# Reading skewed score rows back in two half-height transfers of 128 columns, in a four-layer graph network kernel

## The chip, the cores and the metric

The kernel runs on one core of a Trainium2 chip, as one launch. The metric is device time in microseconds (us) from the first to the last instruction. Before the change three runs gave 2887.09, 2887.32 and 2894.89 us, median 2887.32 us. The profiled execution of the same kernel spans 2889.8 us.

The engines are named as in the profile: PE multiplies matrices (PEld is its weight load), DVE and ACT do elementwise work on vectors, POOL is a slower general engine, and SP only issues transfers. Transfers are carried out by 16 DMA engines, which take a queue's packets in order.

## The reference: what is computed

The input is 128 graphs of 128 nodes with 128 features, and a 0/1 adjacency matrix for each. Four graph layers follow one another, each added to its input after a layer norm and a relu. The change lies in the second layer, which builds attention from pairs of nodes:

```python
D = jnp.abs(x[:, :, None, :] - x[:, None, :, :])
h = jnp.einsum('bijc,oc->bijo', D, W1) + b1
# batch norm of h over all b, i, j, then leaky relu with slope 0.01
s = jnp.einsum('bijo,uo->biju', h, W2)[..., 0] + b2[0]
s = jnp.where(A_init > 0, s, NEG)
A = jax.nn.softmax(s, axis=-1)
y = jnp.einsum('bij,bjc->bic', A, x)
```

For every pair of nodes (i, j) of a graph there is one score, s. It is symmetric in i and j, because D is an absolute difference. So half of the pairs are enough, if the other half is put in place afterwards.

## The kernel before, in words

**Stages.** The first stage (to about 1620 us) computes the first layer, and for the second layer the hidden values h of all pairs, which it stores to DRAM as tensors named hp. Since the batch norm needs statistics over everything, the scores can only be finished in a second pass. That pass is the middle stage (about 1620 to 2400 us): it loads hp back as tiles named z, finishes the scores, and computes attention and the layer's output. The last stage does layers three and four.

**Half of the pairs, by distance.** For node i the kernel keeps only the pairs with the nodes i + 1 to i + 64, counted cyclically (`KH` is 32, so 2 * KH is 64). With the diagonal, a row has 1 + 64 scores. They lie in the tile sk (128 nodes x 4 batches x 65), by distance and not by column.

**Rows of scores.** To turn distance into column, the row of node i is written to DRAM starting at column i. The DRAM buffer rows has 128 rows of `ROW` = 192 columns per batch; the step from row to row in the write is `ROW + 1`, which shifts each row by one. This is `to_rows`, L994. Row i then covers the columns i to i + 64. Those from 128 on stand for columns 0 to 63, since the distance is cyclic. The buffers are set to zero once at the start, and what no row covers stays zero. Two buffers serve the groups by turns (`slots`).

`from_rows`, L1001, reads all 192 columns of all 128 rows back as the tile u. `folded`, L1012, adds the columns 128 to 191 onto the columns 0 to 63. u then holds one half of the score matrix; PE transposes it (`turned("put", t["u"])`, L986), and `scores` adds u and its transpose, L1016, and masks it, L1017. After that come the softmax, the products and the stores of `stored`, L1048 and L1050.

**The order of work.** In the middle stage it is written out by hand. One slot handles one batch (`slot(b)`); four batches are a group, whose chain of steps is spread over twelve slots by `at(slot, place, work)`. In its slot a batch's z tiles get a scale, bias and leaky relu on ACT and DVE (L944, L948, L962), PE multiplies them by the score weights (L919), and two z tiles for later are fetched (`fetch`, L911). Ten z tiles of 1 MB are in the ring (`FETCHED`). For group g, with s0 = 4g + 9, the write to rows is issued in slot s0 - 4, the read in slot s0 - 2, the fold is in slot s0, and the scores are in slot s0 + 1.

**Queues.** All these transfers are issued by SP, in program order: in a group 8 z, one sk, one x load, one u, one x store and (for 24 of 32 groups) one store of y. The read of u waits for the write of sk to land, because it reads what that wrote. What stands behind the read in the program is not issued before it. The issues also take eight completion semaphores by turns, so that each waits for the transfer eight places ahead of it to have landed.

Of the kernel before, what the change touches and what calls it, by code (L numbers as in the profile page):

```python
# [14 lines left out]
OP = mybir.AluOpType  # L15
AX = mybir.AxisListType

P = 128
# [9 lines left out]
KH = 32  # L28
# [138 lines left out]
def tile_gnn_stack(ctx: ExitStack, tc: tile.TileContext, a: dict, out: bass.AP):  # L167
    nc = tc.nc
# [681 lines left out]
    with tc.tile_pool(name="c1", bufs=1) as c1, tc.tile_pool(name="p1", bufs=2) as p1:  # L850
# [22 lines left out]
                                       add_k[:, :, 4:8], op0=OP.mult, op1=OP.add)  # L873


        slots = []
        zero = c1.tile([P, G, ROW], F32, name="zero")
        nc.vector.memset(zero, 0.0)
        for n in range(2):
            rows = dr.tile([G, P, ROW], F32, tag=f"rows{n}", name=f"rows{n}")  # L880
# [4 lines left out]
        for n in range(2):  # L885
            t = c1.tile([P, G, 1 + 2 * KH], F32, name=f"sk{n}")
# [86 lines left out]
        def chain(g):  # L973

            rows = slots[g % 2]
            t = {}
# [21 lines left out]

            def from_rows():
                t["u"] = p1.tile([P, G, ROW], F32, name="u")  # L1000
                nc.sync.dma_start(t["u"], rows.rearrange("g i r -> i g r"))  # L1001

            def normed():
                t["h"] = pre_norm(p1, t["x"], MV1[:, g], RS1[:, g])
# [3 lines left out]
                nc.gpsimd.tensor_tensor(t["x1"], t["x"], over_group(bt), OP.add)  # L1008

            def folded():  # L1010
                u = t["u"]
                nc.vector.tensor_tensor(u[:, :, 0:2 * KH], u[:, :, 0:2 * KH], u[:, :, P:], OP.add)  # L1012

            def scores():
                t["e"] = p1.tile([P, G, P], F32, name="e1")
# [35 lines left out]

            at(s0 - 4, "s", to_rows)
            at(s0 - 2, "s", from_rows)
            at(s0, "e", normed)
            at(s0, "p", lambda: turned("pt", t["h"]))
            at(s0, "l", folded)
            at(s0 + 1, "am", lambda: copied("hT", "pt"))
            at(s0 + 1, "p", lambda: turned("put", t["u"]))
# [511 lines left out]
```

## Time and profile before

| stage, us from the start | DMA, GB/s | PE busy | DVE busy | ACT busy |
|---|---|---|---|---|
| 0 to 1630 | 202 | 1397.8 of 1630 | 1491.1 | 1415.4 |
| 1700 to 2330 | 409 | 546.3 of 630 | 539.5 | 501.9 |
| 2400 to 2890 | 49 | 416.3 of 490 | 387.1 | 386.3 |

The table is from the busy times by stretches. A busy engine is one that executes; waiting is not counted. Matmuls are pipelined and the ends of their records are modelled, so PE's share is a rough one. The DMA share is the mean busy share of the 16 DMA engines.

Over the whole span PE is busy for 85%, DVE for 87% and ACT for 83%, but these are means over stages that differ: only the middle stage loads the DMA engines fully. The chain of work that ended last passes through the transfers z<-hp (7%), rows<-sk (7%) and u<-rows (5% of the span).

### The profile page before, as it was taken

The numbers are of one execution on the slowest core, as the hardware profiler recorded it, in microseconds if no ns is written. First come the engines' busy times: TensorE is split into PE (matmuls) and PEld (weight loads), VectorE is DVE, ScalarE is ACT, GpSimd is POOL, SyncE is SP. The second block draws the span as 40 slices with busy tenths as digits, with TensorE's granted clock in tenths as the row PEclk, the third lists the DMA queues.
The fourth block names the chain that finished last, engine by engine and source line by source line (L and its number), as shares of the span: only waits on it lengthen the run. The fifth ranks groups of instructions, "written<-read, shape, count | busy, mean of one in ns | idle before, by whom it ended". The sixth has DMA issues, their size and how long they took to land.

```text
span 2889.8 us, 41921 instructions
## 1 busy us (share of the span) xinstructions
PE 2469.7 (85%) x14517; PEld 1185.7 (41%) x14517; DVE 2520.0 (87%) x4949; ACT 2392.2 (83%) x2811; POOL 1729.1 (60%) x1613
## 2 busy tenths in 40 slices
PE   1899899999898989898989688888888886998897
PEld 1333333333333333333333234444444444777675
DVE  5799999999999999999999578888888885987886
ACT  1799998989899999999999678777877774988886
POOL 2899989898989899898988001101111104665552
PEclk8899999999999999999999899999999997999998
DMA  5555545454544444454544999999999971111210
GB/s 200 201 202 221 204 190 204 190 204 190 204 193 200 195 199 200 193 207 186 215 171 204 368 408 408 410 409 409 410 410 410 408 283 54 45 59 63 63 34 27
DMA packets 180083, 653.83 MB, mean 226 GB/s; under 512 B 30992, under 2 KB 99472, under 8 KB 129680
## 3 DMA queue, kind: packets, MB, share of 16 engines
q1 hardware_dynamic: 179280, 646.80, 56.3%
q10 hardware_dynamic: 576, 4.19, 0.4%
q8 instruction: 119, 1.95, 0.3%
q14 instruction: 108, 0.88, 0.1%
HBM read 338.14 MB, written 312.80 MB: 225 GB/s over the span
## 4 chain that ended last, share of the span: by engine, by line
PE 36%; ACT 23%; DMA 20%; DVE 12%; issue 5%; POOL 3%; SPq 0%; DVEq 0%; ACTq 0%; POOLq 0%
PE hp L595 17%; ACT d L624 11%; DMA z<-hp 7%; DMA rows<-sk 7%; PE hp L598 5%; ACT hs L608 5%; DMA u<-rows 5%; DVE d L585 3%; PE pv L1292 2%; ACT o L717 2%; PE ps L919 1%; ACT h L1176 1%; DVE z L962 1%; PE po L741 1%; POOL rs L221 1%
## 5 line engine op out<-in xcount | busy, mean ns | idle before, releaser
L585 POOL TENSOR_TENSOR d<-xe 128x2048 f32<-128x2048 f32 x256 | 1074.0, 4201 | 86.2 <-PE hp L595 65.7
L595 PE MATMUL hp<-d,w1T 128*64 128x512 f32 x4096 | 1019.2, 621 | 123.1 <-ACT d L624 65.4
L624 ACT ACTIVATE d<-d 128x2048 f32<-128x2048 f32 x384 | 730.9, 1922 | 9.2 <-POOL d L585 5.0
L585 DVE TENSOR_TENSOR d<-xe,xp 128x2048 f32<-128x2048 f32 x256 | 579.9, 2265 | 28.6 <-PE xp L660 21.2
L608 ACT COPY hs<-hp 128x1024 f32<-128x1024 f32 x512 | 512.1, 1017 | 80.2 <-PE hp L598 43.3
L595 PEld LDWEIGHTS hp<-d,w1T 128*64 128x64 f32 x4096 | 290.9, 142 | 691.7 <-issue 465.3
L1008 POOL TENSOR_TENSOR x<-x,bt 128x512 f32<-128x512 f32 x32 | 43.7, 1366 | 684.7 <-DMA x<-x 684.7
L615 DVE BATCH_NORM_STATS2 st<-hs 128x6 f32<-128x512 f32 x512 | 348.8, 681 | 51.6 <-ACT hs L608 51.6
L616 DVE BATCH_NORM_STATS2 st<-hs 128x6 f32<-128x512 f32 (+1 forms) x512 | 328.7, 642 | 0.0
L962 DVE SCALAR_TENSOR_TENSOR z<-z 128x2048 f32<-128x2048 f32 x128 | 297.0, 2320 | 22.8 <-ACT z L944 22.8
L944 ACT ACTIVATE z<-z,bias,scale 128x2048 f32<-128x2048 f32 x128 | 267.3, 2088 | 18.8 <-DMA z<-hp 18.8
L948 ACT ACTIVATE zr<-z,bias,scale 128x2048 f32<-128x2048 f32 x128 | 267.4, 2089 | 9.7 <-DMA z<-hp 7.5
L598 PE MATMUL hp<-both_t,xw 128*64 128x512 f32 x1024 | 266.2, 594 | 0.0
L919 PE MATMUL ps<-z,w2z 128*32 128x512 f32 x1024 | 141.7, 626 | 83.2 <-DVE z L962 83.2
L926 PEld LDWEIGHTS pk<-pick,su 128*128 128x128 f32 x1024 | 125.7, 193 | 139.9 <-DVE su L940 103.0
L926 PE MATMUL pk<-pick,su 128*128 128x16 f32 x1024 | 138.2, 267 | 25.8 <-DVE su L940 24.7
L1292 PE MATMUL pv<-wr,e 128*128 128x128 f32 x1024 | 148.4, 293 | 10.7 <-DVE e L1269 6.1
L1292 PEld LDWEIGHTS pv<-wr,e 128*128 128x128 f32 x1024 | 133.8, 204 | 19.7 <-issue 3.8
L919 PE MATMUL ps<-z,w2l 128*32 128x512 f32 x1024 | 139.1, 612 | 0.6 <-DMA z<-hp 0.6
L919 PE MATMUL ps<-zr,w2r 128*32 128x512 f32 x1024 | 139.0, 615 | 0.4 <-ACT zr L948 0.4
L598 PEld LDWEIGHTS hp<-both_t,xw 128*64 128x64 f32 x1024 | 78.1, 138 | 143.1 <-issue 142.5
L1269 DVE SCALAR_TENSOR_TENSOR e<-e,ps 128x512 f32<-128x512 f32 x160 | 106.8, 678 | 28.7 <-ACT ps L1266 27.9
(266 smaller groups left out, 3855.5 us busy)
## 6 DMA issues: line engine op xcount, KB each, us to landing
hp<-hs SPq DMA_DIRECT2D x128, 2048.0 KB, 6.3
z<-hp SPq DMA_DIRECT2D x256, 1024.0 KB, 14.8
x<-x SPq DMA_DIRECT2D x128, 256.0 KB, 4.8
u<-rows SPq DMA_DIRECT2D x32, 384.0 KB, 11.6
x<-in_x_dram SPq DMA_DIRECT2D x32, 256.0 KB, 3.0
adj<-in_adj_dram SPq DMA_DIRECT2D x32, 256.0 KB, 3.4
out_dram<-x SPq DMA_DIRECT2D x32, 256.0 KB, 2.5
agg<-a SPq DMA_DIRECT2D x30, 256.0 KB, 3.8
```

Source lines behind the costliest of these rows:

```text
L585: eng.tensor_tensor(d, ahead, x[:, None, None, :].to_broadcast([P, 2, KC, P]), OP.max if t == BY_MAX else OP.subtract)
L595: nc.tensor.matmul(hp[64 * hh:64 * hh + 64, c:c + 512], w1T2 if by_max else w1T, d[:, hh, c:c + 512], start=True, stop=not by_max, skip_gr ...
L598: nc.tensor.matmul(hp[64 * hh:64 * hh + 64, c:c + 512], XW[i // NT // 2][:, i // NT % 2, :], both_t.rearrange("p h k i -> p h (k i)")[:, h ...
L608: nc.scalar.copy(halves[b][:, t, :], linear.pop(i))
L615: nc.vector.bn_stats(st[:, 2 * t, :], hs[:, 0:512])
L616: nc.vector.bn_stats(st[:, 2 * t + 1, :], hs[:, 512:1024 - P * last])
L624: nc.scalar.activation(diffs[i], diffs[i], AF.Abs)
L919: nc.tensor.matmul(ps[32 * c:32 * c + 32, :], w[:, w0:w0 + 32], v[:, 512 * c:512 * c + 512], start=j0 == 0, stop=w is w2r, skip_group_chec ...
L944: nc.scalar.activation(z0, z0, AF.Identity, bias=bias1, scale=scale1[:, 0:1])
L948: nc.scalar.activation(zr, z1, AF.Relu, bias=bias1, scale=scale1[:, 0:1])
L962: nc.vector.scalar_tensor_tensor(z0, z0, 0.01, z0, op0=OP.mult, op1=OP.max)
L1292: nc.tensor.matmul(t[pv][:, k % 2, hd, :], t[e][:, hd, :], flat[:, at:at + P], start=True, stop=True)
```

## The change

Row i covers columns i to i + 64. Rows 0 to 63 therefore never reach beyond column 127, and rows 64 to 127 never use a column below 64. So each half of the rows needs only 128 of the 192 columns. The change reads them as two transfers: rows 0 to 63 with columns 0 to 127, and rows 64 to 127 with columns 64 to 191. It is there to move 256 KB per group in place of 384 KB.

The fold changes with it. For the lower half of the rows there is nothing to fold. For rows 64 to 127 the columns 0 to 63 of u are no longer read from DRAM, so the columns 128 to 191 are copied there in place of being added to zeros; the copy runs on 64 partitions. The tile u, the DRAM buffers and the write of the rows stay as they are.

```diff
             def from_rows():
                 t["u"] = p1.tile([P, G, ROW], F32, name="u")
-                nc.sync.dma_start(t["u"], rows.rearrange("g i r -> i g r"))
+                for i in (0, 64):
+                    nc.sync.dma_start(t["u"][i:i + 64, :, i:i + P],
+                                      rows[:, i:i + 64, i:i + P].rearrange("g i r -> i g r"))
...
             def folded():
-                u = t["u"]
-                nc.vector.tensor_tensor(u[:, :, 0:2 * KH], u[:, :, 0:2 * KH], u[:, :, P:], OP.add)
+                u = t["u"][64:]
+                nc.vector.tensor_copy(u[:, :, 0:2 * KH], u[:, :, P:])
```

## The prediction

> **What bounds the kernel now.** I read the page's slices first, to find which stage holds the change. The edited lines run only in the middle stage, where scores become attention weights; it is the block of nines in the DMA row, slices 22 to 31.
>
> ```profile
> DMA  5555545454544444454544999999999971111210
> GB/s 200 201 202 221 204 190 204 190 204 190 204 193 200 195 199 200 193 207 186 215 171 204 368 408 408 410 409 409 410 410 410 408 283 54 45 59 63 63 34 27
> ```
>
> In that stage the 16 DMA engines move 408 to 410 GB/s; before it half that, after it a seventh. A table by stretches of 160 us inside it (columns: time, busy PE, PEld, DVE, ACT, POOL, PE clock, DMA share, GB/s):
>
> ```profile
> 1860.00:2020.00 160.00, 136.84 (x1062) 65.61 (x1062) 137.72 (x209) 127.50 (x89) 15.35 (x12) 1.00 1.03 409
> ```
>
> PE and DVE are busy for 86%, ACT for 80%, the DMA engines for all of it. (The share passes 1 because packets overlap a little.) In a table by single microseconds, from 1937 to 1986 us, the DMA share never falls below 0.94, so the queue does not run dry between bursts. Next the waits, of the engines and of the DMA-issuing queue SP, over 1700 to 2300 us (total, times, longest):
>
> ```profile
> DVE u L1012 <- DMA u<-rows: 46.5, 26, 3.3
> SPq L1001 <- DMA rows<-sk: 100.8, 25, 5.4
> SPq L994 <- DMA z<-hp: 48.6, 24, 2.4
> ```
>
> No engine waits for the large z transfers themselves; they are fetched ten ahead. What compute waits for is u, which stands behind those z transfers in the one queue: 1.9 us a group. The same window's transfers (KB each, us to landing), and the fold beside a one-source DVE operation of known size:
>
> ```profile
> z<-hp SPq DMA_DIRECT2D x202, 1024.0 KB, 14.7
> u<-rows SPq DMA_DIRECT2D x25, 384.0 KB, 11.6
> rows<-sk SPq DMA_DIRECT2D x25, 130.0 KB, 13.3
> L1012 DVE TENSOR_TENSOR u<-u 128x256 f32<-128x256 f32 x26 | 11.1, 426 | 46.5 <-DMA u<-rows 46.5
> L244 DVE TENSOR_SCALAR hn<-hn 128x512 f32<-128x512 f32 x25 | 10.7, 427 | 0.9
> ```
>
> Landing times of 11 to 15 us for transfers of 0.3 to 2.5 us at 409 GB/s mean some 10 us of work already queued. A group of four batches takes 23.76 us (the issues at L994 go from 1723.9 to 2294.2 in 24 steps). So this stage lasts as long as its DMA work does; taking DMA time out shortens it, taking engine time out does not.
>
> [...] The new rows are exactly 512 B, the old ones 768 B. The trace agrees that nothing bad happens at 512 B: in its records of single packets those of the first stage take 28.3 ns on average (median 27), against 38.3 ns (median 36) for the 768 B ones here. [...] No transfer of some size to half the partitions is in this trace[...]. [...] the trace agrees, 512 elements of one source in 427 ns beside 256 of two sources in 426.
>
> **The change part by part.** *The read.* Now: 512 packets (128 partitions times 4 batches) of 768 B, 512 x 38.3 / 16 engines = 1.23 us of full DMA time a group. After: two transfers of 256 packets of 512 B, 512 x 28.3 / 16 = 0.91 us, or 0.86 at the median of 27 ns. That takes out 0.32 to 0.36 us. The second transfer brings 16 more semaphore packets of 9.4 ns, one per engine: 0.01 us. The packet times of a group sum to 24.4 us against a period of 23.76, so I divide by 1.025: net 0.30 to 0.34 us. The bytes alone say the same: 131 KB less at 409 GB/s is 0.32. I take 0.32. Thirty of the 32 reads meet a full queue (packets seen from 1687 to 2345 us); 30 x 0.32 = 9.6 us.
>
> *The second issue on SP.* 0.37 us like the first (L1001). Behind it in SP's queue stand the two stores (L1048, L1050) and the next four z fetches. SP spends 100.8 us of 600 waiting at L1001 alone, and 10 us of transfers are queued, so it hides. The issues also wait by turns on eight semaphores, each for the transfer eight places earlier: that is what L994 waits for when it names z. Fourteen transfers a group in place of 13 shift this by one place. L994 will then wait for the first half of u, 0.3 us after the z that it waits for now. With the four small ones in flight, at least three z, 3.1 MB, or 7.7 us of work, stay queued; the engines still never run dry. Cost: nothing, with 0.1 us a group (3 us) as the upper end.
>
> *The fold.* A 64-partition copy in place of the add. At the one-source rate of L244, 256 elements take between 290 ns[...] and the 426 of now: 0 to 4 us of DVE over 32 groups. DVE has 14% idle and 1.9 us a group of waiting on u just before, so it is worth nothing in the full stage.
>
> *The tail.* The last two or three groups meet an emptying queue (u lands in 3.6 to 4.0 us); a second issue may add 0.4 us each, of which the fold gives back 0.1. DVE waits for u only once there, 1.2 us. I put +0.5.
>
> Sum: 2887.3 - 9.6 + 0.5 = 2878.2, so 2878. The bounds 0.30 and 0.34 give 2877.5 to 2879; with the 3 us for SP's order, 2881.
>
> **The rivals.** *B, no change, 2888.* [...] The saving is eaten whole; what is left is the semaphores and the tail, +0.8. For it: [...]that all the transfers share one FIFO. Against it: a half is only 16 packets, 8 KB, per engine, 0.45 us. The packet records show that the engines are not in step (the 512 packets of one u are spread over 3.3 us early in the stage and 9.7 us late), so one engine's half meets other engines' z, and short collisions may be absorbed. The same time comes out if the chain S to u (13.3 + 11.6 us, about one period) sets the pace rather than the bytes; against that stands the full DMA share.
>
> *C, slower, 2903.* If every packet of a half takes twice its time[...], the read costs 512 x 56.6 / 16 = 1.81 us, 0.57 more after the same division; 30 x 0.57 = 17 us, less if it is partly absorbed: 2892 to 2904. [...] For it: these are the fullest 650 us of the kernel, with no slack.[...]
>
> **How the numbers follow.** A, the bytes count: 0.54, of which 0.42 lies beyond 0.3% (8.7 us), since its centre of 9 is near that line. B, [...]: 0.25, nearly all within 0.3%. C: 0.21. So faster 0.42, same 0.36, slower 0.22. The range holds A with its bounds, from 2875 (packets at the median and a little from the earlier u), all of B, and C up to half, 2898.
>
> **What would show it.** Right: u<-rows with 64 issues of 128 KB, packets of 512 B near 28 ns, the same 408 to 410 GB/s, a period of 23.45 us, the fold near 0.3 us, the other stages unchanged. B would show as the same period at about 404 GB/s, C as a longer one with packets of 512 B or of z taking visibly longer than 28 and 315 ns. Wrong would be any change outside 1620 to 2400 us, or a DMA share under 1 in the stage: then SP's order, which I cost at nothing, starves the engines.

## The result and the profile after

The changed kernel takes 2923.74 us (median of four runs, 2920.34 to 2926.84) against 2888.2 before (the three runs above and one more). The ratio is 1.012, with a 95% interval of 1.0104 to 1.0137: slower by some 35 us, where 2878 was forecast.

The page's slices of the changed kernel, DMA share and rate:

```profile
DMA  5554544545444444544445999999999981112110
GB/s 201 203 215 195 202 192 197 209 186 214 191 198 198 191 198 196 210 195 205 201 180 213 391 386 392 389 387 381 375 389 374 388 299 56 44 55 66 62 34 27
```

The same stage is full as before, but at 374 to 392 GB/s where it was 408 to 410. The stretch that the prediction showed (time, busy PE, PEld, DVE, ACT, POOL, PE clock, DMA share, GB/s), then the waits and the transfers of 1700 to 2300 us, and the fold:

```profile
1860.00:2020.00 160.00, 140.69 (x1006) 67.26 (x1002) 126.73 (x197) 119.00 (x84) 15.32 (x13) 0.93 1.03 384
```

```profile
DVE u L1015 <- DMA u<-rows: 64.5, 24, 4.2
SPq L1003 <- DMA rows<-sk: 79.8, 24, 5.0
SPq L995 <- DMA u<-rows: 10.1, 21, 0.6
```

```profile
z<-hp SPq DMA_DIRECT2D x191, 1024.0 KB, 13.8
u<-rows SPq DMA_DIRECT2D x48, 128.0 KB, 12.6
```

```profile
L1015 DVE COPY u<-u 64x256 f32<-64x256 f32 x24 | 7.0, 291 | 64.5 <-DMA u<-rows 64.5
```

Three things stand in these lines. The DMA share is 1.03 in both kernels: the engines never starve, so the order of issues is not what is wrong; L995 now waits for u, as foreseen, at most 0.6 us. DVE and ACT do less work in the same 160 us (DVE 126.7 against 137.7), so the stage runs slower as a whole. And engines that are busy all the time move fewer bytes per us, so single packets must take longer. The records of single packets between 1700 and 2300 us, mean ns, and the period of a group (mean of the 26 from the third issue of the sk write to the 29th) show where:

| kernel | u packets | z, 8192 B | x and y, 2048 B | period, us |
|---|---|---|---|---|
| before | 38.3 (768 B) | 315.1 | 90.2 | 23.76 |
| changed | 38.2 (512 B) | 333.0 | 95.0 | 25.23 |

A packet of u is a third smaller and takes as long as before. The z packets, which the change does not touch, became slower by 18 ns in the mean; their median stayed at 313, but the slowest 5% went from over 321 to over 447 ns. That is some packets held up for long, not all a little. The first stage is unchanged (ACT busy for 1407 us up to 1620 us in both).

### The profile page after: what moved, and what is told of

Read it like the earlier page. It is cut to its first block, busy times and chain, and to the rows that moved or that the text cites. A ratio compares the mean times of both kernels' runs of the same rounds, so it can differ in the third digit from the quotient of the medians.

```text
span 2925.0 us, 42008 instructions
## 1 busy us (share of the span) xinstructions
PE 2494.3 (85%) x14517; PEld 1195.0 (41%) x14517; DVE 2513.9 (86%) x4949; ACT 2391.1 (82%) x2811; POOL 1719.8 (59%) x1613
## 4 chain that ended last, share of the span: by engine, by line
PE 33%; DMA 25%; ACT 22%; DVE 11%; issue 5%; POOL 4%; SPq 0%; DVEq 0%; ACTq 0%; POOLq 0%
PE hp L595 16%; DMA u<-rows 11%; DMA rows<-sk 11%; ACT d L624 10%; PE hp L598 5%; ACT hs L608 5%; DVE d L585 3%; PE pv L1295 2%; ACT o L717 2%; DMA z<-hp 1%; ACT h L1179 1%; PE po L741 1%; POOL d L585 1%; DVE e L1272 1%; PE ph L735 1%
## 5 line engine op out<-in xcount | busy, mean ns | idle before, releaser
L1011 POOL TENSOR_TENSOR x<-x,bt 128x512 f32<-128x512 f32 x32 | 45.5, 1423 | 732.9 <-DMA x<-x 620.3
L920 PE MATMUL ps<-zr,w2r 128*32 128x512 f32 x1024 | 146.4, 645 | 0.3 <-ACT zr L949 0.3
```

The lines of the kernel that those rows point to most:

```text
L920: nc.tensor.matmul(ps[32 * c:32 * c + 32, :], w[:, w0:w0 + 32], v[:, 512 * c:512 * c + 512], start=j0 == 0, stop=w is w2r, skip_group_chec ...
```

## The experiments

The theory to test: a transfer that goes to only half of the partitions delays the z packets of the same queue (*position*), in which the 326 transfers issued between 1700 and 2300 us landed in the order of their issue before the change. A transfer whose partitions lie all in 0 to 63, or all in 64 to 127, is called one-sided below, and is said to collide with z where it delays z's packets. What in the hardware would make it do so, no trace here shows. In the expectations the figures that bear no rival's name are the theory's. The rivals: the additional transfer and its place in the order of semaphores; packets of 512 B; the copying fold.

**The pieces apart, first four runs.** In *e1*, two transfers again, but each of full height:

```diff
-                nc.sync.dma_start(t["u"], rows.rearrange("g i r -> i g r"))
+                for k in (0, 2):
+                    nc.sync.dma_start(t["u"][:, k:k + 2, :], rows[k:k + 2].rearrange("g i r -> i g r"))
```

> The read of u is two transfers as in the changed kernel, but each covers all 128 partitions (two batches each, 192 columns, 768 B packets), with the old adding fold. [...] 2888, within 4 us of before. Rival, the second issue and its place in the order of eight semaphores: about 2920, as in the changed kernel or above it, since here no bytes are saved.

Measured: 2886.58 us, ratio 1.0001 (0.9992 to 1.001). The second issue costs nothing that can be seen.

*e2*, small packets at full height:

```diff
-                nc.sync.dma_start(t["u"], rows.rearrange("g i r -> i g r"))
+                nc.sync.dma_start(t["u"][:, :, 0:P], rows[:, :, 0:P].rearrange("g i r -> i g r"))
...
-                u = t["u"]
-                nc.vector.tensor_tensor(u[:, :, 0:2 * KH], u[:, :, 0:2 * KH], u[:, :, P:], OP.add)
+                u = t["u"][64:]
+                nc.vector.tensor_copy(u[:, :, 0:2 * KH], u[:, :, 2 * KH:P])
```

> One transfer of all 128 partitions with 512 B packets (columns 0 to 127); the scores that wrap past column 127 are left out, and the fold copies columns 64 to 127 instead, at the same size. [...] the bytes saved come through, 2878 (2876 to 2881), z packets at 315 ns. Rival, that 512 B packets or the copy are what is slow: 2910 or more.

Measured: 2878.76 us, 0.997 (0.9959 to 0.9981). Packets of u take 28.0 ns, those of z 315.6, and the period is 23.49. This fits the forecast's own sum, 2878, for a kernel in which the transfer keeps its height; by the interval the saving is 5 to 12 us.

*e3*, half height with the bytes and the fold of before:

```diff
-                nc.sync.dma_start(t["u"], rows.rearrange("g i r -> i g r"))
+                for i in (0, 64):
+                    nc.sync.dma_start(t["u"][i:i + 64], rows[:, i:i + 64, :].rearrange("g i r -> i g r"))
```

> Two transfers of 64 partitions each, all 192 columns, with the old adding fold: half height, but the bytes and packets of before. [...] 1.5 times the half-height bytes of the changed kernel, whose collisions cost 45 us over the byte saving; so some 2888 + 1.5 x 45 = 2955 (2930 to 2975). Rival, packet size: 2888. Rival, the extra issue: about 2920 to 2930.

Measured: 2958.3 us, 1.024 (1.0223 to 1.0257): 70 us for the same bytes in the same packets, split by partition. The packets of u take 56.3 ns in place of 38, those of z 341.1.

*e4*, also 64 partitions each, but every second one (the fold as in e2):

```diff
-                nc.sync.dma_start(t["u"], rows.rearrange("g i r -> i g r"))
+                for i in (0, 1):
+                    nc.sync.dma_start(t["u"][i::2, :, 0:P], rows[:, i::2, 0:P].rearrange("g i r -> i g r"))
```

> Two transfers of 64 partitions of 512 B packets, but of the even and of the odd partitions[...]; data as in the full-height run (wrapping scores left out). [...] 2878 to 2890. [...] 2905 to 2925, as in the changed kernel.

Measured: 2880.23 us, 0.9974 (0.9967 to 0.9981); packets of u 27.6 ns, of z 315.6. Twice 64 partitions, twice 128 KB, and no loss. So here it is not the number of partitions, but which. (The lower range expected was for a loss that goes by which partitions are reached, the upper for one that every half has.)

The same stretch in e2, e3 and e4, one line each:

```profile
1860.00:2020.00 160.00, 140.72 (x1082) 67.53 (x1086) 139.05 (x214) 129.63 (x90) 12.96 (x12) 0.99 1.03 409
```

```profile
1860.00:2020.00 160.00, 133.65 (x967) 63.24 (x965) 119.60 (x186) 116.61 (x83) 14.25 (x12) 0.94 1.03 370
```

```profile
1860.00:2020.00 160.00, 142.51 (x1086) 69.48 (x1086) 137.49 (x209) 128.41 (x89) 16.77 (x13) 0.98 1.03 409
```

The share is 1.03 in all three, and only the rate tells them apart: 409, 370, 409. A full DMA share does not say that the bytes flow at full rate.

**The other parts, and kernels that may gain.** *e5* is the fold's edit of the change alone.

> The read of before (one transfer, 192 columns), with the fold by a copy on 64 partitions alone. [...] the fold is not on the path, 2888 within 4 us. Rival, the copy has a part in the loss: 2895 or more.

Measured: 2891.12 us, 1.0002 (0.9995 to 1.001). The copy takes 291 ns, and DVE's wait for u before it is about as it was, 44.3 us in all against 46.5:

```profile
L1012 DVE COPY u<-u 64x256 f32<-64x256 f32 x26 | 7.6, 291 | 44.3 <-DMA u<-rows 44.3
```

*e6* uses what e4 suggests, that which partitions a transfer reaches decides. The 64 partitions from 32 on lie on both sides of the middle, and rows 32 to 95 need just 128 columns. That this position loses nothing was an assumption when e6 was built.

```diff
+        whole = []
+        for n in range(2):
+            whole.append(c1.tile([P, G, ROW], F32, name=f"u{n}"))
+            nc.vector.memset(whole[n], 0.0)
...
-                t["u"] = p1.tile([P, G, ROW], F32, name="u")
-                nc.sync.dma_start(t["u"], rows.rearrange("g i r -> i g r"))
+                t["u"] = whole[g % 2]
+                for i, n, w in ((32, 64, 128), (0, 32, 96), (96, 32, 96)):
+                    nc.sync.dma_start(t["u"][i:i + n, :, i:i + w],
+                                      rows[:, i:i + n, i:i + w].rearrange("g i r -> i g r"))
...
-                nc.vector.tensor_tensor(u[:, :, 0:2 * KH], u[:, :, 0:2 * KH], u[:, :, P:], OP.add)
+                for i, w in ((32, 32), (64, 32), (96, 64)):
+                    u = t["u"][i:i + 32]
+                    nc.vector.tensor_copy(u[:, :, 0:w], u[:, :, P:P + w])
```

> Three transfers: rows 32 to 95 with columns 32 to 159 (64 partitions[...], 128 KB), rows 0 to 31 with columns 0 to 95 and rows 96 to 127 with columns 96 to 191 (32 partitions each,[...] 48 KB each). 160 KB less than before, worth 12 to 13 us; 96 KB of one-sided transfers in place of the 256 KB of the changed kernel, at 45 us per 256 KB worth 17 us. [...] 2892 (2882 to 2900). Rival, any transfer of less than 128 partitions costs: 2925 or more.

Measured: 2885.23 us, 0.9985 (0.9978 to 0.9991): some 4 us under the kernel before, though most of its saving of 12 to 13 us is lost again. The middle's packets of 512 B take 27.4 ns, as without a loss in e4 (27.6); those of z 319.3, a quarter of the changed kernel's delay. The one-sided 96 KB cost about 8 us where 17 were expected.

*e7* asks whether stores suffer too:

```diff
-                to = rows[0, 0, 0:1]
-                nc.sync.dma_start(bass.AP(tensor=to.tensor, offset=to.offset,
-                                          ap=[[ROW + 1, P], [P * ROW, G], [1, 1 + 2 * KH]]), sk[g % 2])
+                for i in (0, 64):
+                    to = rows[0, i, i:i + 1]
+                    nc.sync.dma_start(bass.AP(tensor=to.tensor, offset=to.offset,
+                                              ap=[[ROW + 1, 64], [P * ROW, G], [1, 1 + 2 * KH]]), sk[g % 2][i:i + 64])
```

> All as before, but the write of sk to DRAM is issued as two transfers of 64 partitions each, 65 KB each. If one-sided transfers that read the on-chip memory collide as those that write it do: 130 KB at 45 us per 256 KB, so 2888 + 23 = 2911. If stores do not collide with the z loads: 2888 within 4 us.

Measured: 2887.36 us, 0.9992 (0.9983 to 1.0001). Reading the on-chip memory by halves, for a store, costs nothing here; the packets of sk take 19.0 ns as before.

*e8* makes only the wrapped columns a half-height transfer (fold as in the change):

```diff
-                nc.sync.dma_start(t["u"], rows.rearrange("g i r -> i g r"))
+                nc.sync.dma_start(t["u"][:, :, 0:P], rows[:, :, 0:P].rearrange("g i r -> i g r"))
+                nc.sync.dma_start(t["u"][64:, :, P:], rows[:, 64:, P:].rearrange("g i r -> i g r"))
```

> One transfer of 128 partitions with columns 0 to 127, and one of partitions 64 to 127 with columns 128 to 191 alone (64 KB, 256 B packets), with the copying fold. Bytes and packets: 9.6 us less for the first, some 8.6 more for the second (256 packets of about 18 ns). One-sided bytes a quarter of those of the changed kernel: 11 us. [...] 2898 (2890 to 2905). Rival, the cost goes by the number of one-sided transfers (one of two): 2908 or more.

Measured: 2897.43 us, 1.0029 (1.002 to 1.0037). That fits a cost by one-sided bytes (2898 expected), and not one by the number of such transfers (2908 or more).

**Which positions lose.** *e9* is e6 with a wider middle:

```diff
-                for i, n, w in ((32, 64, 128), (0, 32, 96), (96, 32, 96)):
+                for i, n, w in ((16, 96, 160), (0, 16, 80), (112, 16, 80)):
...
-                for i, w in ((32, 32), (64, 32), (96, 64)):
-                    u = t["u"][i:i + 32]
-                    nc.vector.tensor_copy(u[:, :, 0:w], u[:, :, P:P + w])
+                u = t["u"][64:]
+                nc.vector.tensor_copy(u[:, :, 0:2 * KH], u[:, :, P:])
```

> As the run with the middle rows, with a wider middle: rows 16 to 111 with columns 16 to 175 (96 partitions,[...] 240 KB), rows 0 to 15 and 112 to 127 with 80 columns each (16 partitions,[...] 20 KB each). Packets of 640 B at some 32 ns and 320 B at some 21: 0.94 us a group against 1.23, so 8 us less. One-sided bytes 40 KB against 96: if the cost goes by the one-sided bytes (some 8 us for the 96 KB), 3.5 us. [...] 2884, 4 to 5 us under before.[...]

Measured: 2917.05 us, 1.01 (1.0075 to 1.0124). This missed by 33 us. The 640 B packets of the middle take 45.5 ns in the mean, with 32 at the fifth percentile, so the transfer that I had called free, since it lies on both sides of the middle, loses too. Why 96 partitions from 16 on lose where 64 from 32 on did not isn't shown. The z packets take 327.3 ns; how much of that the middle causes, and how much the two ends, the packet records don't tell.

*e10* sends both halves of the changed kernel to one side (u lies in two tiles zeroed once, as in e6):

```diff
-                for i in (0, 64):
-                    nc.sync.dma_start(t["u"][i:i + 64, :, i:i + P],
-                                      rows[:, i:i + 64, i:i + P].rearrange("g i r -> i g r"))
+                for i, to in ((0, t["u"][0:64, :, 0:P]), (64, other)):
+                    nc.sync.dma_start(to, rows[:, i:i + 64, i:i + P].rearrange("g i r -> i g r"))
```

> The two half-height transfers of the changed kernel, with the same bytes and packets, both to partitions 0 to 63: the second goes to a spare tile, so the scores of the rows 64 to 127 are left out. If the two halves of the changed kernel relieve each other[...], the time goes up, to 2935 or more, since now one side takes all 256 KB. If each half costs by itself[...]: 2924, within 5 us of the changed kernel.

Measured: 2927.55 us, 1.0136 (1.0118 to 1.0154), which the noise doesn't tell from the changed kernel's 1.012. The two halves hardly relieve each other; each costs by itself.

*e11* leaves the kernel before as it is and adds one unused transfer, at partition 0, 16 or 32. Here 16; the others differ in that number alone:

```diff
                 nc.sync.dma_start(t["u"], rows.rearrange("g i r -> i g r"))
+                nc.sync.dma_start(zero[16:80, :, 0:P], rows[:, 16:80, 0:P].rearrange("g i r -> i g r"))
```

> All of before, and after the read of u one more transfer that nothing uses: 64 partitions from partition 0 on, 256 packets of 512 B. Its bytes alone are worth 0.44 us a group, 13 us. Half of the changed kernel's one-sided bytes: 0.87 us a group more, 26 us. So 2888 + 39 = 2927 (2918 to 2936).

> The same extra transfer, to the 64 partitions from partition 16 on. [...] as from partition 0, about 2927. [...] a third of that loss, 2910.

> The same extra transfer, to the 64 partitions from partition 32 on[...]. [...] only the bytes, 2901 (2897 to 2906). Rival, any transfer of 64 partitions costs: 2927 as from partition 0.

Measured: 2920.49 us from partition 0 on (1.011, 1.0093 to 1.0127), 2923.21 from 16 on (1.0117, 1.01 to 1.0134), and 2899.13 from 32 on (1.0032, 1.0019 to 1.0044). The transfer is the same one three times. From 32 on it costs its bytes, 10 us (128 KB at 409 GB/s are 0.32 us a group); from 0 or 16 on it costs three times as much, and about the same for both. So lying on both sides of the middle is not enough: the transfer from 16 on does, with 48 partitions below it and 16 above, and loses as much as the one from 0 on. The stretch for 16 and for 32:

```profile
1860.00:2020.00 160.00, 135.72 (x1010) 64.47 (x1013) 130.00 (x200) 120.14 (x83) 24.21 (x14) 0.96 1.03 396
```

```profile
1860.00:2020.00 160.00, 136.35 (x1056) 65.61 (x1052) 133.91 (x207) 125.04 (x87) 26.78 (x14) 0.99 1.03 407
```

The runs together give a measure, an estimate made after them. Count the KB that a group moves by transfers to the positions that lose (one-sided ones, and those from 16 on); and take as loss what a run takes beyond its bytes, at 9.6 us per 128 KB in the whole kernel:

| run | KB a group to such positions | loss, us | us per 128 KB |
|---|---|---|---|
| changed kernel | 256 | 45 | 23 |
| e3 | 384 | 70 | 23 |
| e6 | 96 | 8 | 11 |
| e8 | 64 | 9 to 13 | 18 to 26 |
| e9 | 280 (middle 240, ends 40) | 34 | 16 |
| e10 | 256 | 47 | 23 |
| e11 from 0, from 16 | 128, 128 | 22, 25 | 22, 25 |

e1, e2, e4 and e11 from 32 on have 0 KB and lose nothing beyond 2 us. Most of the others lose some 23 us per 128 KB. At that rate the 40 KB that e9's expectation counted would cost 7 us; the other 27 would be the middle's, 14 us per 128 KB, but the two were not measured apart. e6 falls out. (e8's loss depends on whether its packets of 256 B are priced by bytes or by packet.)

## Why the prediction was wrong

**Right: the bound.** The stage lasts as long as its DMA work. Every run that took DMA time away without one-sided transfers became faster, and every one that added it slower.

**Right, with the height kept: the sum for the read.** e2 and e4 give 2878.76 and 2880.23 against the forecast 2878, with packets of 28 ns. The steps for the second issue on SP (e1) and for the fold (e5) hold as well: both cost nothing that can be seen, though an issue of a half takes 0.60 us and not the 0.37 of the prediction. The fold takes 291 ns, close to the 290 of the prediction, which two lines of the trace before also give, as an estimate: L244 takes 427 ns for 512 elements a partition and L935 154 ns for one, and 154 + 255 x (427 - 154) / 511 = 290.

**Wrong: "short collisions may be absorbed".** That is the argument with which the prediction set aside a loss by halves and gave 0.54 to the bytes alone. The runs show the opposite: e3 loses 70 us with unchanged bytes, and the z packets themselves are delayed (341.1 ns in place of 315.1). That the packets of one u are spread over 3.3 us and more did not protect them. So the step that failed is the sum for the read: it took out 0.32 us a group for u's packets and put the delay of everything else at nothing. Measured, the other packets cost 1.27 us a group more, and u's own 0.32, so that the saving was gone and 1.27 us came on top.

**Wrong: rival C's size.** C came nearest, but put 2903 at 0.21. Its working doubled the time of u's packets and left their effect on z without a number. Measured, u's packets account for (38.2 - 28.3) x 512 / 16 = 0.32 us a group, where C had 0.91; z's for (333.0 - 315.1) x 1024 / 16 = 1.15 us, where C had nothing; x and y for 0.12. The term that was mis-sized is z: a delay of 6% on 86% of the bytes (8.4 of 9.7 MB a group). Together with the saving these make 1.3 us of the measured 25.23 - 23.76 = 1.47 us a group. The remaining 0.2 us lie in where the periods begin and end: between those issues the trace has 1039 z packets a group in the changed kernel and 1028 before, where a group needs 1024. Counted by 1024 z packets between 1700 and 2300 us, a group takes 24.93 us against 23.69, 1.24 more, which the sum gives too (1.27 / 1.025).

**Rival B was wrong about what a half costs.** That two halves would take just as long as the read of before, 1.23 / 1.025 = 1.20 us, was the author's estimate, and the delay of the other packets was not in it. It makes 0.60 us for a half, 0.28 beyond the 0.32 of its bytes. e11 has 24.95 us a group from partition 0 on and 24.28 from 32 on: 0.67 us beyond its bytes for one half, more than twice as much. Its other ground, a pace set by the chain from the sk write to u, doesn't fit either: the DMA share is 1.02 or 1.03 in the stretch from 1860 us on in every run, which leaves no time in which the engines wait for a chain.

**What stays open.** That the loss goes by position is shown: the same transfer costs 10 us from partition 32 on, and 31 and 34 us from 0 and from 16 on. What in the hardware makes it so isn't shown, nor which engines serve which partitions, since the packet records carry no engine. Nor is the source tested apart: the rows read from DRAM move along with the partitions in every run but e10, and no run reads rows 32 to 95 into partitions 0 to 63. Nor is it clear why e6's 96 KB cost half of what most of the others give by the KB.

## What to carry to other kernels

When the DMA engines are the bound, cost a transfer by the partitions that it goes to as well as by its bytes. Here a load cut by partitions 0 to 63 and 64 to 127 lost 45 us where it was to save 9.6, and 1.27 of the 1.59 us that it lost a group came to the other transfers in the queue. If a load must be cut, these cuts lost nothing beyond 2 us: by batches (e1, 2886.58 us), to fewer columns at full height (e2, 2878.76), or by even and odd partitions (e4, 2880.23). The 64 partitions from 32 on are such a piece too (e11, 10 us for 128 KB), but what then remains on either side of them is one-sided, and lost some 8 us in e6. A DMA share of 1.03 at 384 GB/s in place of 409 is the sign to look for in a profile: busy engines that move less. Smaller packets move less a ns too: in e2 those of 512 B take 28.0 ns, 18 B a ns, and those of 8192 B 315.6 ns, 26 B a ns. So look at how long packets of one size take.

## What the runs showed of the hardware that was not expected

- Where a transfer's partitions begin decided in e11: 64 partitions from 32 on were free of the loss (z packets at 315.8 ns, 2899 us), 64 from 16 on were as bad as 64 from 0 on (2923 and 2920 us).
- Stores from half the partitions didn't show it (2887.36 us in e7), with the same z loads in flight.
- The slowest 1% of the z packets take over 613 ns in the changed kernel, against over 331 before: twice a packet's usual 313.
